# A constant row for the Gram matrix: spread over partitions by a DRAM transfer instead of by matmuls

## The chip, the cores and the metric

The kernel runs on one NeuronCore of a Trainium2 chip. The metric is device time in microseconds (us) of one execution. Names of the engines: PE is TensorE (PEld its weight loads), DVE is VectorE, ACT is ScalarE, POOL is GpSimd, SP is SyncE, which here only issues DMAs. "SPq" in a row of the profile is SyncE's queue issuing one.

## What is computed

The reference is two residual bottleneck blocks, one after the other, on 64 images of 1024 channels and 14 x 14 pixels, in float32:

```
out = relu(bn(conv1x1(x,   w1) + b1, g1, be1))      # 1024 -> 256 channels
out = relu(bn(conv3x3(out, w2) + b2, g2, be2))      # 256 -> 256
out = bn(conv1x1(out, w3) + b3, g3, be3)            # 256 -> 1024
x   = relu(x + softplus(residual_scale) * out)
```

`bn` takes mean and variance of a channel over all images and pixels (12544 values), then scales and shifts.

## The kernel before

`y_all` holds the 256 middle channels of all 12544 pixels in SBUF, as two slots of 128 channels (128 partitions). A block goes through these stages: the first 1x1 convolution and its statistics, the 3x3 convolution (`conv2`, by a Winograd scheme) with its statistics, the Gram stage, and the last 1x1 convolution with the residual, which in the first block is interleaved with the first convolution of the second block. The loop `for b in range(2)` (L1638) runs the last three stages of each block.

**The Gram stage** serves the statistics of the last convolution: mean and variance of its 1024 output channels follow from the 256 x 256 matrix of products of the middle channels, summed over pixels, and from their sums. `gram` (L1119) forms it on TensorE. A matmul sums over partitions, so pixels must stand on partitions; `y` is transposed, 256 pixels at a time, into tiles `zt` (six buffers), and each `zt` takes part in 16 matmuls (the rows cp<-zt and ap<-zt). There are 49 `zt` in a Gram. A constant per channel, `minus_c` (L1641, minus the positive part of the parameter `be2`), is added to `y` first.

- `by_tensor` (L1203): eight of the 49 `zt` come from TensorE: four transposes against `ident` into PSUM (L1208), then one VectorE addition that takes the result out of PSUM and adds the constant (L1215). After the transpose channels lie along the free dimension, so the constant is needed as a row of 256 values, the same in all 128 partitions: `c_row`.
- `by_vector` (L1221): the other 41 are transposed by VectorE in 32 x 32 blocks (L1224). For that the pixels are first moved between groups of 32 partitions: `less` subtracts the constant in place (L1166), then `move` issues DMAs of 80 or 96 KB from SyncE and GpSimd (L1187) and `stay` copies the parts that keep their partitions on ScalarE. The moves go to three buffers `homes` in turn.

**How `c_row` is made before.** `center_row` (L1194) multiplies `minus_c`, broadcast along the free dimension, by the identity, one matmul per slot, which gives the row in all partitions of a PSUM tile of the tag "ax"; ScalarE copies it to SBUF. After the first `by_tensor`, `busy(psum, "ax", 1)` issues one filler matmul of 448 columns.

**The order.** Within an engine the order of the work around this place is the program's: a call of `tc.keep_in_program_order` pins an instruction behind the one traced before it on its engine. Instructions that aren't pinned are placed by the framework's scheduler as soon as it takes them for ready. `pairs` (L1231) sets the order of the Gram: it normalises the first pixels, makes the row, and then, between one `by_tensor` and the next, normalises, subtracts and moves the rest by a list written out by hand. Its first steps on VectorE are: normalise two slices of 256 pixels, `zt` 0, normalise 512 pixels, `zt` 1, subtract from the first moved piece (the moves follow), `zt` 2.

On SyncE, ahead of the Gram, stand the loads of weights: `load_w3` (L170, 1 MB) in both blocks, and `load_w1` (L144, 1 MB in four pieces) in the first block only, for the second block's first convolution.

**Memory.** Tiles come from pools. A pool whose memory another pool held before waits, by default, for all that used the earlier pool; with `reuse_waits="tile"` each tile waits only for what lay at its own place. `homes` are tiles of the pools that later hold `x`; the third one, `homes[2]`, comes from the pool `last_x_{b}`.

Of the kernel before, what the change touches and what calls it, by code (L numbers as in the profile page):

```python
# [38 lines left out]
FP = mybir.dt.float32  # L39
AF = mybir.ActivationFunctionType  # L40
ALU = mybir.AluOpType

P = 128
N, C, H, W = 64, 1024, 14, 14
HW = H * W
M = 256
CS = C // P
MS = M // P
# [42 lines left out]
def bottlenecks(ctx: ExitStack, tc: tile.TileContext, x, w1s, w2s, w3s, pars, out):  # L91
    nc = tc.nc
# [3 lines left out]
    dram = ctx.enter_context(tc.tile_pool(name="dram", bufs=1, space=bass.MemoryType.DRAM))  # L96
# [76 lines left out]
    def matmul(*args, **kw):  # L173

        tc.keep_in_program_order(nc.tensor.matmul(*args, **kw))  # L175

    def busy(psum, tag, n, with_=None):

        v = ident if with_ is None else with_
        for i in range(n):  # L180
            matmul(psum.tile(448, tag), v, v[:, :1].to_broadcast([P, 448]), start=True, stop=True)
# [154 lines left out]
    def act(*args, **kw):  # L336

        tc.keep_in_program_order(nc.scalar.activation(*args, **kw))  # L338
# [247 lines left out]
    def norm_vector(s, y, aff):  # L586

        scale, shift = aff
        tc.keep_in_program_order(
            nc.vector.tensor_scalar(y, y, scale[:, s : s + 1], shift[:, s : s + 1], ALU.mult, ALU.add)  # L590
        )
        tc.keep_in_program_order(nc.vector.tensor_scalar(y, y, 0.0, None, ALU.max))
# [523 lines left out]
            )  # L1116
        return ps

    def gram(psum, pool, homes, aff, minus_c, beside):  # L1119

# [66 lines left out]
                )  # L1189
                tc.keep_in_program_order(ins)  # L1190

        c_row = pool.tile([P, M], FP, tag="c_row", name="c_row")

        def center_row():  # L1194

            ps = psum.tile(M, "ax")
            for s in range(MS):
                matmul(
                    ps[:, s * P : (s + 1) * P], minus_c[:, s : s + 1].to_broadcast([P, P]), ident, start=True, stop=True
                )  # L1200
            act(c_row, ps, AF.Copy)

        def by_tensor(a):  # L1203
            tp = psum.tile(CH * M)
# [26 lines left out]
        def pairs():  # L1231

            for a in 0, px:
                norm_vector(1, y_all[:, 1, a : a + px], aff)
                normed(a, a + px, (0,))
            normed(2 * px, 4 * px, (0,))
            center_row()
            rest = [(piece, s) for piece in still for s in range(MS)]
            (second, end), half = still[1], sum(still[1]) // 2
            for n, a in enumerate(a for piece in still for a in range(*piece, px)):  # L1240
                yield by_tensor(a)
                if n == 0:
                    busy(psum, "ax", 1)
                    norm_vector(1, y_all[:, 1, 2 * px : 4 * px], aff)
                    normed(*moved[0])
                elif n == 1:
                    less(*moved[0])
                    move(0)
                    normed(second, end, (0,))
                    normed(second, half, (1,))  # L1250
                elif n == 3:
                    norm_vector(1, y_all[:, 1, half:end], aff)
                    normed(*moved[1])
                elif n == 4:
                    less(*moved[1])
                    move(1)
                    normed(*moved[2])
                elif n == 5:
                    less(*moved[2], both[:1])
                    stay(1)  # L1260
                elif n == 6:
                    less(*moved[2], both[1:])
                    normed(*moved[3])
                elif n == 7:
                    move(2)
                    stay(2)
            for k, (a, e) in enumerate(moved):
                for i in range((e - a) // px):
                    yield by_vector(k, i)
                    if i in (1, 3) and k and k + 2 < len(moved):  # L1270
                        less(*moved[k + 2], both[i // 2 : i // 2 + 1])
                        if i == 3:
                            move(k + 2)
                            if k + 3 < len(moved):
                                normed(*moved[k + 3])
                            stay(k + 2)
                    elif i in (0, 5) and k > 1 and rest:
                        piece, s = rest.pop(0)
                        less(*piece, (s,))
            assert not rest  # L1280
# [302 lines left out]
    ident = keep.tile([P, P], FP, tag="ident", name="ident")  # L1583
# [12 lines left out]
    with tc.tile_pool(name="first", bufs=1) as one, tc.tile_pool(  # L1596
        name="first_x", bufs=2
    ) as x_left, ExitStack() as scope:
        xpools = x_right, x_left
        psum = Psum(scope, ["ps"], ps=4, ay=2)  # L1600
# [4 lines left out]
        for b in range(2):  # L1605
            p = keep.tile([P, NPAR], FP, tag=f"par{b}", name=f"par{b}")
# [31 lines left out]
    for b in range(2):  # L1638
        pb = par[b]
        minus_c = keep.tile([P, MS], FP, tag="minus_c", name="minus_c")  # L1640
        nc.vector.tensor_scalar(minus_c, pb[:, BE2 : BE2 + MS], 0.0, -1.0, ALU.max, ALU.mult)  # L1641
        stats2 = keep.tile([P, MS, 1 + PARTS, nc.vector.BN_STATS_DIM], FP, tag="stats2", name=f"stats2_{b}")
        with tc.tile_pool(name=f"conv2_{b}", bufs=1, reuse_waits="tile") as pool, ExitStack() as scope:
            border.go_on(Psum(scope, ["l"], l=2, m=2), pool, stats2)

        if b == 0:
            x_right, x_scope = right_pool("last_x_right")
        with tc.tile_pool(name=f"last_{b}", bufs=1) as one, tc.tile_pool(
            name=f"last_x_{b}", bufs=2 if b == 0 else 5
        ) as x_left:  # L1650
            xpools = (x_right, x_left) if b == 0 else (x_left, x_left)
            w3 = load_w3(one, b)
            if b == 0:
                w1 = load_w1(one, b + 1, nc.sync)
            aff = affine(aggregate(stats2, 0), pb, G2, BE2)
            with ExitStack() as scope:
                if b == 0:
                    psum = Psum(scope, ["cy", "ay", "cx", "cy", "ay"], cy=2, ay=2)
                else:
                    psum = Psum(scope, ["cy", "cx"], cy=2, cx=2, cp=2)  # L1660
                with tc.tile_pool(name=f"gram_{b}", bufs=1) as pool:
                    def x_tile(name, t=0):
                        return xpools[t].tile([P, CS * PX], FP, tag="x", name=name)


                    ws = sums_tile(one, 2 - b)
                    homes = [x_tile("home"), x_tile("home") if b else ws.rearrange("p i n -> p (i n)"), x_tile("home", 1)]

                    made_c, made_a = [], []
                    beside = {NPX // (CH * P) - 10: lambda: made_c.append(combine_w3(w3, ws[:, 0]))}  # L1670
                    if b == 0:
                        beside[NPX // (CH * P) - 4] = lambda: made_a.append(combine_w1(w1, ws[:, 1]))
                    grams = gram(psum, pool, homes, aff, minus_c, beside)

                    made = [conv3(psum, 0, 0, w3, "cx" if b else "ay")]
                    mv3 = small.tile([P, CS, nc.vector.BN_AGGR_DIM], FP, tag="mv3", name="mv3")
                    conv3_stats(psum, pool, grams, w3, mv3, ("cy", "cp", "cy", "cp" if b else "cx"), homes[2])
                made.append(conv3(psum, 0, 1, w3, "cx" if b else "ay"))
                tags = ("cy", "cp") * 2 if b else ("cy", "cx", "cy")
                made += [conv3(psum, 0, 2 + i, w3, tag) for i, tag in enumerate(tags)]  # L1680
                if b == 0:
                    psum.cycle = itertools.cycle(["ay", "ay", "cy"])
                aff = affine(mv3, pb, G3, BE3, conv_bias=B3)
                for a in aff:
                    nc.vector.tensor_scalar(a, a, sps[b], None, ALU.mult)
                xs = [load_x(xpools[t % 2], b, t, run=tc.keep_in_program_order) for t in range(2 if b == 0 else 5)]
                later = None if b else []
                residual(psum, xs[0], b, 0, w3, aff, made, later)
                weights = made_a + made_c
                with tc.tile_pool(name=f"rest_{b}", bufs=1) as pool:  # L1690
                    if b == 1:
                        final(psum, pool, x_left, xs, w3, *weights, aff)
                        return
                    stats1 = stats_tile(MS, f"stats1_{b + 1}")
                    border = Border(b + 1, stats1, x_scope)
                    fused(psum, pool, xpools, xs, *weights, aff, par[b + 1], stats1, border, later)
# [40 lines left out]
```

## Time and profile before

| | us |
|---|---|
| three runs | 1922.47, 1921.18, 1922.40 |
| median | 1922.40 |
| profiled execution, its time | 1922.36 |
| its span, from the first to the last instruction | 1920.6 |
| TensorE busy in the span | 1903.6 |
| the first Gram's first `zt` (L1215) starts at | 587.66 |
| the second Gram's first `zt` starts at | 1541.86 |

A row of the timeline has the start and the length in us, engine, line, operation, the tile written and the tiles read, the shape, and how often it is repeated in the row; in square brackets stand the idle time ahead of it and what ended that. A row of waits has who waited for whom, the total in us, how often, and the longest. Fp32 matmuls appear as two passes each. A row of DMA issues has the tile written and read, the queue, the count, the size of one and the median time from issue to landing in us. A row of windows has the window, its length, the busy time of PE, PEld, DVE, ACT and POOL (with instruction counts), the granted TensorE clock as a share, the busy share of the 16 DMA engines, and GB/s.

### The profile page before, as it was taken

The numbers are of one execution on the slowest core, as the hardware profiler recorded it, in microseconds if no ns is written. First come the engines' busy times: TensorE is split into PE (matmuls) and PEld (weight loads), VectorE is DVE, ScalarE is ACT, GpSimd is POOL, SyncE is SP. The second block draws the span as 40 slices with busy tenths as digits, with TensorE's granted clock in tenths as the row PEclk, the third lists the DMA queues.
The fourth block names the chain that finished last, engine by engine and source line by source line (L and its number), as shares of the span: only waits on it lengthen the run. The fifth ranks groups of instructions, "written<-read, shape, count | busy, mean of one in ns | idle before, by whom it ended". The sixth has DMA issues, their size and how long they took to land.

```text
span 1920.6 us, 28737 instructions
## 1 busy us (share of the span) xinstructions
PE 1903.6 (99%) x10236; PEld 1598.3 (83%) x10236; DVE 1547.1 (81%) x2509; ACT 1085.6 (57%) x2152; POOL 565.5 (29%) x678
## 2 busy tenths in 40 slices
PE   9999999999999999999999999999999999999999
PEld 5555557999998799999999999989999987555555
DVE  5787767999998866676776767789999986888886
ACT  2222214677778255555555555556777682666665
POOL 0111100211204133433433333302121041666664
PEclk9999999999999999999999999999999999999999
DMA  7767644787856544444444444358778466889998
GB/s 290 274 241 279 218 154 155 195 223 212 216 168 172 192 159 169 169 168 181 178 179 168 168 169 178 124 179 204 216 209 221 141 171 240 292 325 337 337 341 300
DMA packets 198527, 408.77 MB, mean 213 GB/s; under 512 B 37104, under 2 KB 175024, under 8 KB 181872
## 3 DMA queue, kind: packets, MB, share of 16 engines
q1 hardware_dynamic: 159712, 321.85, 48.9%
q0 software_dynamic: 33056, 34.03, 8.6%
q10 hardware_dynamic: 5616, 51.06, 6.4%
q8 instruction: 81, 1.33, 0.3%
q14 instruction: 62, 0.51, 0.1%
HBM read 263.75 MB, written 115.34 MB: 197 GB/s over the span
## 4 chain that ended last, share of the span: by engine, by line
PE 90%; DVE 5%; DMA 2%; issue 1%; SPq 1%; POOL 1%; ACT 1%; DVEq 0%; ACTq 0%; POOLq 0%
PE cy L175 17%; PE ay L175 17%; PE columns L175 13%; PE cp L175 10%; PE ap L175 9%; PE m L175 7%; PE l L175 6%; PE cx L175 5%; PE ax L175 4%; PE ps L175 1%; DMA home<-y 1%; SPq L1187 1%; DVE zt L1224 1%; DVE y L1166 1%; DMA x<-in_x 1%
## 5 line engine op out<-in xcount | busy, mean ns | idle before, releaser
L338 ACT ACTIVATE cu<-cy,scale 128x196 f32<-128x196 f32 (+1 forms) x552 | 256.7, 474 | 278.0 <-PE cy L175 272.8
L175 PE MATMUL columns<-v,ub 128*128 128x224 f32 (+1 forms) x1536 | 302.4, 338 | 0.8 <-ACT columns L338 0.8
L338 ACT ACTIVATE x<-x,shift 128x392 f32<-128x392 f32 x452 | 255.0, 613 | 72.7 <-POOL x L530 53.6
L175 PEld LDWEIGHTS columns<-v,ub 128*128 128x128 f32 x1536 | 269.2, 188 | 5.7 <-ACT columns L338 1.5
L504 DVE SCALAR_TENSOR_TENSOR x<-cp,scale,x 128x196 f32<-128x196 f32 (+1 forms) x368 | 178.1, 484 | 96.6 <-PE cp L175 95.2
L175 PE MATMUL cy<-ct,ws 128*128 128x196 f32 (+1 forms) x736 | 221.8, 383 | 1.2 <-ACT cu L338 1.2
L175 PE MATMUL ay<-at,ws 128*128 128x196 f32 (+1 forms) x768 | 212.8, 382 | 0.2 <-ACT au L338 0.2
L525 POOL TENSOR_TENSOR x<-x,cu 128x196 f32<-128x196 f32 (+1 forms) x184 | 160.0, 870 | 171.7 <-ACT cu L338 163.9
L530 POOL TENSOR_TENSOR x<-x,cu 128x392 f32<-128x392 f32 x124 | 125.9, 1015 | 191.3 <-DVE x L504 191.3
L175 PEld LDWEIGHTS ay<-at,ws 128*128 128x128 f32 x768 | 139.2, 190 | 35.0 <-ACT au L338 0.8
L175 PEld LDWEIGHTS cy<-ct,ws 128*128 128x128 f32 x736 | 133.4, 190 | 36.4 <-ACT cu L338 4.2
L175 PE MATMUL l<-diffs,ub 128*128 128x224 f32 (+1 forms) x768 | 149.8, 337 | 3.7 <-issue 2.6
L551 POOL TENSOR_TENSOR x<-x,cu 128x392 f32<-128x392 f32 x120 | 122.0, 1017 | 86.2 <-DVE x L504 66.1
L175 PE MATMUL m<-sums,ua 128*128 128x224 f32 (+1 forms) x752 | 146.2, 337 | 0.5 <-DVE sums L667 0.4
L175 PEld LDWEIGHTS l<-diffs,ub 128*128 128x128 f32 x768 | 134.2, 189 | 6.0 <-issue 3.3
L338 ACT ACTIVATE au<-ay 128x196 f32<-128x196 f32 (+1 forms) x140 | 53.4, 382 | 146.4 <-PE ay L175 146.0
L504 DVE SCALAR_TENSOR_TENSOR x<-cx,scale,x 128x196 f32<-128x196 f32 (+1 forms) x184 | 89.1, 484 | 56.7 <-PE cx L175 56.7
L175 PEld LDWEIGHTS m<-sums,ua 128*128 128x128 f32 x752 | 131.3, 189 | 2.3 <-DVE sums L667 1.7
L175 PE MATMUL cy<-y,w 128*128 128x196 f32 (+1 forms) x408 | 125.3, 393 | 0.0
L175 PE MATMUL cx<-y,w 128*128 128x196 f32 (+1 forms) x400 | 122.6, 391 | 0.0
L175 PE MATMUL cp<-y,ws 128*128 128x196 f32 (+1 forms) x368 | 113.6, 390 | 0.2 <-DVE x L504 0.2
L965 POOL DMA_DIRECT2D y<-f x24 | 30.8, 1490 | 274.4 <-DVE f L889 272.5
(239 smaller groups left out, 3996.9 us busy)
## 6 DMA issues: line engine op xcount, KB each, us to landing
x<-in_x SPq DMA_DIRECT2D x62, 1568.0 KB, 6.8
ub<-u SPq DMA_DIRECT2D x92, 768.0 KB, 5.4
x<-mid SPq DMA_DIRECT2D x32, 1568.0 KB, 8.4
mid<-x ACTq DMA_DIRECT2D x31, 1568.0 KB, 5.1
out<-x SPq DMA_DIRECT2D x123, 392.0 KB, 5.9
ua<-u SPq DMA_DIRECT2D x92, 256.0 KB, 3.1
u<-y POOLq DMA_DIRECT2D x48, 256.0 KB, 6.8
home<-y SPq DMA_DIRECT2D x70, 96.0 KB, 3.7
```

What stands on the lines that cost most here:

```text
L175: tc.keep_in_program_order(nc.tensor.matmul(*args, **kw))
L338: tc.keep_in_program_order(nc.scalar.activation(*args, **kw))
L504: nc.vector.scalar_tensor_tensor(v, bank, self.scale[:, o : o + 1], v, ALU.mult, ALU.add)
L525: nc.gpsimd.tensor_add(self.part(1, 1), self.part(1, 1), u3)
L530: nc.gpsimd.tensor_add(v, v, self.u12)
L551: nc.gpsimd.tensor_add(v, v, self.u12[:, i * self.n : (i + 1) * self.n])
L965: nc.gpsimd.dma_start(out=out_rows[3][:, o], in_=fa[:, o, :full], accum_op=ALU.add)
L1166: tc.keep_in_program_order(nc.vector.tensor_scalar(y, y, minus_c[:, s : s + 1], None, ALU.add))
L1187: ins = queue.dma_start(out=x[32 * i : 32 * i + 32, :, j], in_=y_all[32 * j : 32 * j + 32, :, a + i * run : a + i * run + run])
L1224: nc.vector.transpose(zt[:, :, 1 : M + 1].rearrange("p b (n c) -> p b n c", c=32), x[:, :, i * CH * 32 : (i + 1) * CH * 32].rearrange("p n ...
```

## The change

The row is no longer made by TensorE and ScalarE. At the head of each block, right after `minus_c`, GpSimd issues a DMA that writes the 256 values to DRAM in channel order. In `gram`, SyncE issues a DMA that reads these 1 KB once for each of the 128 partitions; it is pinned to the program's order. The row goes to the first 256 columns of `homes[2]`, not to a tile of its own. The filler matmul after the first `by_tensor` goes too. The pool `last_x_{b}`, from which `homes[2]` comes, gets `reuse_waits="tile"`.

```diff
-    def gram(psum, pool, homes, aff, minus_c, beside):
+    def gram(psum, pool, homes, aff, minus_c, c_dram, beside):
...
-        c_row = pool.tile([P, M], FP, tag="c_row", name="c_row")
-
-        def center_row():
-
-            ps = psum.tile(M, "ax")
-            for s in range(MS):
-                matmul(
-                    ps[:, s * P : (s + 1) * P], minus_c[:, s : s + 1].to_broadcast([P, P]), ident, start=True, stop=True
-                )
-            act(c_row, ps, AF.Copy)
+        c_row = homes[2][:, :M]
+        tc.keep_in_program_order(
+            nc.sync.dma_start(out=c_row, in_=bass.AP(c_dram.tensor, c_dram.offset, [[0, P], [1, M]]))
+        )
...
             normed(2 * px, 4 * px, (0,))
-            center_row()
...
                 if n == 0:
-                    busy(psum, "ax", 1)
                     norm_vector(1, y_all[:, 1, 2 * px : 4 * px], aff)
...
         nc.vector.tensor_scalar(minus_c, pb[:, BE2 : BE2 + MS], 0.0, -1.0, ALU.max, ALU.mult)
+        c_dram = dram.tile([M], FP, tag=f"c{b}", name=f"c{b}")
+        nc.gpsimd.dma_start(out=c_dram.rearrange("(s p) -> p s", p=P), in_=minus_c)
...
-            name=f"last_x_{b}", bufs=2 if b == 0 else 5
+            name=f"last_x_{b}", bufs=2 if b == 0 else 5, reuse_waits="tile"
         ) as x_left:
...
-                    grams = gram(psum, pool, homes, aff, minus_c, beside)
+                    grams = gram(psum, pool, homes, aff, minus_c, c_dram, beside)
```

## The prediction

> **What bounds the kernel now.** I read the busy times first, then TensorE's waits, then the timeline of each engine around the two places where the row is made (the first Gram at 586 us, the second at 1540 us), then SyncE's queue and the DMA windows there.
>
> ```profile
> PE 1903.6 (99%) x10236; PEld 1598.3 (83%) x10236; DVE 1547.1 (81%) x2509; ACT 1085.6 (57%) x2152; POOL 565.5 (29%) x678
> ...
> PE ax L175 <- ACT c_row L338: 1.0, 2, 0.5
> ...
> PE cp L175 <- DVE zt L1224: 0.7, 3, 0.3
> ```
>
> TensorE has work for 1903.6 of 1920.6 us, so a change counts only by how it moves TensorE. Its whole wait for the row is 1.0 us in two waits: what the change can win there is of that order. But the row also holds up VectorE, which starts the moves of `y` for the rest of the Gram. The first Gram, TensorE and then VectorE:
>
> ```profile
> 586.11 0.61 PE L175 MATMUL ax<-ident,minus_c 128*128 128x128 f32 x4
> 586.55 0.60 PE L1208 MATMUL cy<-ident,y 128*128 128x128 f32 x4
> 587.63 1.02 PE L175 MATMUL ax<-ident 128*128 128x448 f32 x2 [0.48 <-ACT c_row L338]
> 588.49 0.60 PE L1208 MATMUL ay<-ident,y 128*128 128x128 f32 x4
> 589.02 0.55 PE L175 MATMUL cp<-zt 128*64 128x193 f32 x4
> ...
> 586.74 0.29 DVE L592 TENSOR_SCALAR y<-y 128x256 f32<-128x256 f32 x1
> 587.66 0.69 DVE L1215 TENSOR_TENSOR zt<-cy,c_row 128x512 f32<-128x512 f32 x1 [0.63 <-ACT c_row L338]
> ```
>
> The reader should see that VectorE is free at 587.03 and the transposes end at 587.15, but the first `zt` starts only at 587.66, when ScalarE has copied the row. The second Gram is the same picture 954.2 us later (`zt` at 1541.86). What the new transfer meets, first SyncE's queue, then the landing times of the 1024 KB and the last two 256 KB weight loads of the first Gram and of the one load of the second, then DMA windows (last two columns: DMA share, GB/s):
>
> ```profile
> 581.02 0.36 SPq L170 DMA_DIRECT2D w<-in_w  x1
> 581.42 2.09 SPq L144 DMA_DIRECT2D w<-in_w  x4
> ...
> w<-in_w SPq DMA_DIRECT2D x1, 1024.0 KB, 4.8
> ...
> w<-in_w SPq DMA_DIRECT2D x2, 256.0 KB, 5.9
> ...
> w<-in_w SPq DMA_DIRECT2D x1, 1024.0 KB, 5.0
> ...
> 587.00:588.00 1.00, 0.52 (x3) 0.30 (x2) 0.37 (x2) 1.00 (x3) 0.00 (x0) 1.00 0.95 367
> 588.00:589.00 1.00, 1.00 (x6) 0.50 (x4) 0.97 (x3) 1.00 (x2) 0.00 (x0) 1.00 0.17 66
> ...
> 1539.00:1540.00 1.00, 1.00 (x4) 0.45 (x3) 0.89 (x7) 0.30 (x1) 0.53 (x6) 1.00 0.41 172
> ```
>
> At the first Gram 2 MB of weights (`w3`, and `w1` in four pieces) keep the DMA engines full until 588.2; at the second only `w3` is loaded, and they are idle from 1539.4. And what stands later in each Gram:
>
> ```profile
> 601.95 3.08 DVE L1224 STREAM_TRANSPOSE zt<-home 128x512 f32<-128x512 f32 x5 [1.05 <-DMA ws<-y]
> ...
> 602.72 0.55 PE L175 MATMUL cp<-zt 128*64 128x193 f32 x4 [0.28 <-DVE zt L1224]
> ...
> 1561.47 1.30 DVE L1224 STREAM_TRANSPOSE zt<-home 128x512 f32<-128x512 f32 x2 [2.95 <-DMA home<-y]
> ...
> 1562.24 0.55 PE L175 MATMUL cp<-zt 128*64 128x193 f32 x4
> ```
>
> The `zt` made from moved pixels wait for DMAs, and TensorE catches up with them: at 602.72 by 0.28 us, at 1562.24 by 0.29 us (the matmuls of before start at 1561.73 and would go on at 1561.95). So each Gram moves by what the moves move by.
>
> **What the Trainium skill says.** "DMA: Bandwidth & Descriptors", section "Queues, rings and completion order": SyncE owns one ring on each DMA engine, and on each engine descriptors are consumed in ring order. The trace agrees: the last 256 KB piece lands 5.9 us after its issue, longer than the 1 MB load issued first on an idle ring (4.8). The same page, "Rules for kernel authors": a strided last dimension takes one descriptor per element; that is the new write of 256 floats. No such transfer is in this trace. "TensorE: Matmul & The Clock Gate", Part 1: after an idle window of about 3.4 us the clock halves until a busy window has passed. Here gaps of up to 1.6 us (the wait list's longest) left the granted clock at 1.00; a longer gap isn't shown.
>
> **The change part by part.**
>
> *Removed.* Per Gram: two fp32 matmuls in four passes (586.11 to 586.55), the ScalarE copy (363 ns), the 448-column filler in two passes (587.63 to 588.49). With the row at hand the second Gram would run so: transposes wait for VectorE's first `y` (ends 1540.57) instead of the matmuls, so 1540.6 to 1541.2; VectorE is free at 1541.23 (0.94 + 0.29); first `zt` at about 1541.27 against 1541.86, a gain of 0.59. Everything behind it on VectorE up to the subtraction (L1166) that releases the moves is back to back, so the moves start 0.59 earlier. TensorE itself gains more: second transposes 1541.3 to 1541.9, Gram at 1542.0 against 1543.21, 1.2 us. But that surplus ends in the DMA wait at 1561.47, where the DMA share has been 0.9 to 1.07 since the moves began: there only the 0.6 of the moves is left.
>
> *Added, the DRAM write.* On GpSimd's queue, 256 elements of 4 bytes. GpSimd's issues here take 0.54 (L1187) to 1.49 us (L965); I take 1.5. `minus_c` is ready at 10.1 us, where GpSimd is idle from 1.3 to 51.7, and for the second block at 631.8, where at most the last moves (the last issued at 632.88) stand behind it and then nothing until 670.28. Those moves may slip by 1.5 us; SyncE's last ones, issued at 633.70 to 635.5, land after them anyway. Cost 0; if that cover were gone, 1.5 us on one Gram.
>
> *Added, the row transfer.* 128 rows of 1 KB. It is pinned on SyncE behind what was traced there before it, and that is `w3`, and in the first block all four pieces of `w1`. Its own wait for the write is long over. `reuse_waits="tile"` lets it wait only for what lay at its place; the last conv2 reads are over at 583, so it costs and gains nothing beyond SyncE's order.
>
> First Gram: issue at 583.5 (581.42 + 2.09), ring busy until 588.2; 128 KB at 350 GB/s is 0.37 us; the last weight piece landed at 583.1 + 5.9 = 589.0, some 0.8 after its data, so the row lands at 588.2 + 0.37 + 0.8 = 589.4. First `zt` at 589.4 against 587.66: **1.75 us later**. Bounds: 588.9 if it lands with the weights (+1.3), 590.4 if 1 KB rows go at a third of the rate (+2.8). Behind the waiting `zt` on VectorE stand the norm of the next slice and the subtraction before the moves, so all moves start 1.75 later. TensorE, waiting for `zt`, starts Gram at 590.15 against 589.02, 1.1 later, but meets the DMA wait again: the moved `zt` comes at 601.95 + 1.75, its matmul at 602.72 + 1.73 = 604.45. From there TensorE is without a wait but for 0.17 us, so 1.73 stays.
>
> Second Gram: issue at 1535.65, ring busy until 1539.4, landing 1539.4 + 0.37 + 0.8 = 1540.6. Wanted at 1541.27: 0.67 to spare, so the whole 0.6 is won. Bounds: -0.6 to +0.5 (the row at 1541.6 to 1542.4).
>
> *Moved.* `c_row` in `homes[2]` is overwritten by the third move and by ScalarE's copies, which follow the last `zt` that reads it (600.22 to 600.9; the move from 601.47): 0. ScalarE runs 0.3 us ahead, behind which nothing waits.
>
> **Sum.** The profiled execution took 1922.36 us, 1.76 more than its span and 0.04 under the median of the three runs, 1922.4. 1922.36 + 1.73 - 0.6 = **1923.5**. The gain of one Gram is outweighed by the lateness in the other; next late is the move chain, as now.
>
> **Rivals.**
> - *The row is in time in both Grams* (the transfer slips past the weights, or weights drain sooner). Then both gain 0.6: 1922.36 - 1.2 = 1921.2. For it: the row was made to come early. Against it: the DMA share of 0.95 to 0.99 until 588 and the ring order. 13%.
> - *The late row lets TensorE's clock fall* in the first Gram. TensorE would idle from 587.7 to 590.15, 2.4 us. It decides at 3.4 us (the page's window), that is, a row that lands at 590.4 or later, or at a lower limit than the page's. Then VectorE is 2.8 late and TensorE 2.2; at half clock for one to two windows (3.4 to 6.8 us) it loses another 1.7 to 3.4, say 2.55, which gives 4.75 on TensorE, less the 0.28 it waits at 602.72: 4.45. The second Gram's gain is then 0.1, as its row is 1 us later too. 1922.36 + 4.35 = 1926.7. For it: all 128 rows read the same 1 KB of DRAM, which no row of this trace does. Against it: the 1.6 us gaps. 12%.
> - *Nothing visible*: the row comes with the weights' end in the first Gram (+1.3) and part of it is regained in slack that I don't see: about 1922.5. 10%.
>
> **How the numbers follow.** The forecast's case has 65%, its own range 1922.4 to 1924.7. No change means within 0.2% (3.8 us), which is about what a measurement of this kernel can tell: 1918.6 to 1926.2. The clock case lies mostly above it, 0.11 with some mishap in the order of other instructions; nothing reaches below it but that, 0.02; the rest is 0.87. The range runs from the in-time case, 1921.2, to just short of the clock case, 1926.2. It leaves out the clock case's 11%, the 2%, and the lower half of the in-time case, 6%.
>
> **What would show it.** In the profile after: the row's issue at about 583.5 and 1535.6, its landing about 589.4 and 1540.6 (the second pair 1.73 later, as all of it is); first `zt` at 589.4, waiting for a DMA, in the first Gram, and in the second at 1543.0 (1541.27 + 1.73), waiting for none; the moves 1.75 later in the first and 0.6 earlier (after that shift) in the second; a TensorE gap of 2.4 us with the clock at 1.00. It is wrong if the row is issued ahead of the weights, if a PE clock under 1.00 stands after the gap, or if either Gram's first move shifts by something other than its first `zt` does.

## The result, and the profile after

| | before | after |
|---|---|---|
| median of six runs each | 1922.42 us (1921.18 to 1923.04) | 1930.3 us (1927.8 to 1932.13) |
| profiled execution | 1922.36 | 1931.22 |
| its span | 1920.6 | 1929.4 |

The ratio of after to before is 1.004, with a 95% interval of 1.003 to 1.0051: slower by 7.9 us, outside the range of the prediction. The loss isn't where the prediction worked. The page's busy times and the longest waits of TensorE say so at once (who waited for whom, total in us, how often, the longest):

```profile
PE 1905.9 (99%) x10224; PEld 1598.1 (83%) x10224; DVE 1547.7 (80%) x2509; ACT 1084.6 (56%) x2150; POOL 564.6 (29%) x680
...
PE ay L175 <- DVE at L438: 3.4, 1, 3.4
PE cp L175 <- DVE zt L1209: 2.8, 2, 2.7
PE cp L175 <- DVE zt L1218: 2.7, 2, 2.4
```

TensorE has fewer matmul passes than before (10224 against 10236) and is busy 2.3 us longer: some run at a lower granted clock, as the windows further down show. Its three new waits of over 2 us stand in three places. Only the second, on the `zt` of the late row (L1209), was forecast; the first is at the start of the kernel, 550 us ahead of the row.

**Where the time goes.** Marks in the two timelines, each the start of a named instruction:

| mark | before | after | shift |
|---|---|---|---|
| conv2 of block 1 begins (first ls<-l) | 316.30 | 320.94 | +4.64 |
| `w3` issued ahead of the first Gram | 581.02 | 585.65 | +4.63 |
| first `zt` of the first Gram | 587.66 | 594.18 | +6.52 |
| first `zt` made from moved pixels | 601.95 | 608.38 | +6.43 |
| the first Gram's result is read (g<-cp) | 648.19 | 659.06 | +10.87 |
| `w3` issued ahead of the second Gram | 1535.27 | 1546.12 | +10.85 |
| first `zt` of the second Gram | 1541.86 | 1552.13 | +10.27 |
| the second Gram's result is read | 1602.33 | 1611.73 | +9.40 |
| span | 1920.6 | 1929.4 | +8.8 |

So: +4.63 before any Gram, +1.8 to +1.9 at the head of the first Gram, +4.4 in the rest of it, -1.5 in the second (-0.6 of it at its head), and -0.6 after it (sum +8.8). The terms at the two heads are close to those of the sum on record (+1.73, -0.6). The two large ones stand beside the two DRAM writes.

**The start of the kernel.** The issues of the first 40 us, the loads of `x` before and then after, and the write; then windows, first of before and then of after (last three columns: granted TensorE clock, DMA share, GB/s):

```profile
x<-in_x SPq DMA_DIRECT2D x5, 1568.0 KB, 10.0
...
x<-in_x SPq DMA_DIRECT2D x5, 1568.0 KB, 16.5
...
c<-minus_c POOLq DMA_DIRECT2D x1, 1.0 KB, 12.6
```

```profile
16.00:18.00 2.00, 2.00 (x8) 1.17 (x7) 1.03 (x2) 0.59 (x1) 0.00 (x0) 1.00 0.97 414
18.00:20.00 2.00, 2.00 (x8) 1.17 (x7) 0.00 (x0) 0.00 (x0) 0.00 (x0) 1.00 1.02 433
20.00:22.00 2.00, 2.00 (x8) 1.17 (x7) 0.00 (x0) 0.00 (x0) 0.00 (x0) 1.00 0.95 406
22.00:24.00 2.00, 2.00 (x8) 1.17 (x7) 0.60 (x1) 0.00 (x0) 0.00 (x0) 1.00 0.99 409
...
14.00:16.00 2.00, 2.00 (x8) 1.17 (x7) 2.00 (x4) 0.44 (x1) 0.00 (x0) 1.00 1.77 408
16.00:18.00 2.00, 2.00 (x8) 1.17 (x7) 0.65 (x2) 0.59 (x1) 0.00 (x0) 1.00 1.03 100
18.00:20.00 2.00, 2.00 (x8) 1.17 (x7) 0.00 (x0) 0.00 (x0) 0.00 (x0) 1.00 1.00 138
20.00:22.00 2.00, 2.00 (x8) 1.17 (x7) 0.00 (x0) 0.00 (x0) 0.00 (x0) 1.00 0.69 75
22.00:24.00 2.00, 2.00 (x8) 1.17 (x7) 0.00 (x0) 0.00 (x0) 0.00 (x0) 1.00 0.40 88
```

GpSimd issues the write at 10.02 in 0.87 us, but its 1 KB lands 12.6 us later, and while it is under way all DMA engines of the core together move 75 to 138 GB/s, where before they move 406 to 433 in the same windows. The loads of `x`, which are issued on another queue and share no data with the write, take 16.5 us to land instead of 10.0. Who waits for them: VectorE before, then VectorE and TensorE after:

```profile
23.40 1.79 DVE L437 TENSOR_TENSOR at<-x 128x1568 f32<-128x1568 f32 x1 [5.44 <-DMA x<-in_x]
...
29.88 1.79 DVE L437 TENSOR_TENSOR at<-x 128x1568 f32<-128x1568 f32 x1 [12.21 <-DMA x<-in_x]
...
35.69 4.57 PE L175 MATMUL ay<-at,ws 128*128 128x392 f32 x8 [3.44 <-DVE at L438]
```

VectorE's first `at` comes 6.48 us later. TensorE has work queued for some microseconds, then stands for 3.44.

The trace's records of single packets say what the DMA engines do meanwhile. (A window counts a packet whole where it starts, so a share over 1, as in 14 to 16, means packets that last beyond the window.) The write goes out as 16 packets of 64 bytes, which start between 14.25 and 15.82 and take 0.025 us each. After that it is the packets of the loads of `x`, 12544 bytes each, that last long: of those that start between 14 and 26 us none takes over 0.49 us before, and 33 take over 1 us after, the longest 6.33.

**The end of the first Gram.** The second write is issued at 640.18, when the last moves of `y` are under way. Windows of after, then VectorE and TensorE, which make the Gram's last `zt` from these moves and multiply them:

```profile
644.00:646.00 2.00, 2.00 (x34) 1.82 (x32) 0.67 (x2) 0.00 (x0) 0.00 (x0) 1.00 1.73 55
646.00:648.00 2.00, 2.00 (x34) 1.79 (x30) 0.00 (x0) 0.00 (x0) 0.00 (x0) 1.00 0.94 50
648.00:650.00 2.00, 0.32 (x6) 0.07 (x2) 0.04 (x1) 0.00 (x0) 0.00 (x0) 1.00 0.10 13
650.00:651.00 1.00, 0.28 (x2) 0.28 (x4) 1.00 (x2) 0.00 (x0) 0.00 (x0) 0.85 0.28 50
651.00:652.00 1.00, 1.00 (x10) 0.82 (x10) 1.00 (x3) 0.00 (x0) 0.00 (x0) 0.50 0.80 301
```

```profile
649.96 1.90 DVE L1218 STREAM_TRANSPOSE zt<-home 128x512 f32<-128x512 f32 x3 [5.29 <-DMA home<-y]
...
650.73 0.92 PE L175 MATMUL cp<-zt 128*64 128x193 f32 x4 [2.41 <-DVE zt L1218]
```

The write lands after 8.9 us, at 649.12; the rate is 13 to 55 GB/s for six of them, where before, from 638 to 644, it was 347 to 427. The two moves that SyncE issues behind the write, at 640.46 and 642.04, land at 649.29 and 649.45, just after the write, though the records of the moves' packets end at 644.43; the moves issued ahead of it have landed by 644.55. VectorE waits 5.29 us for the last moved pixels and TensorE 2.41; the clock column then shows half speed.

**The head of the first Gram.** SyncE's issues, then VectorE and TensorE, then windows:

```profile
585.65 0.36 SPq L170 DMA_DIRECT2D w<-in_w  x1
586.06 2.16 SPq L144 DMA_DIRECT2D w<-in_w  x4
588.26 0.43 SPq L1194 DMA_DIRECT2D home<-c  x1
```

```profile
594.18 0.69 DVE L1209 TENSOR_TENSOR zt<-cy,home 128x512 f32<-128x512 f32 x1 [2.51 <-DMA home<-c]
...
594.93 0.55 PE L175 MATMUL cp<-zt 128*64 128x193 f32 x4 [2.65 <-DVE zt L1209]
...
596.20 1.12 PE L1202 MATMUL cx<-ident,y 128*128 128x128 f32 x4
597.25 0.91 PE L175 MATMUL cp<-zt 128*64 128x193 f32 x4
```

```profile
595.00:596.00 1.00, 1.00 (x16) 0.92 (x16) 0.97 (x3) 1.00 (x2) 0.00 (x0) 1.00 0.00 0
596.00:597.00 1.00, 1.00 (x10) 0.72 (x4) 1.00 (x2) 1.00 (x2) 0.00 (x0) 0.54 0.00 0
597.00:598.00 1.00, 1.00 (x8) 0.59 (x8) 1.00 (x3) 1.00 (x2) 0.00 (x0) 0.50 0.00 0
598.00:599.00 1.00, 1.00 (x10) 0.86 (x8) 0.58 (x1) 1.00 (x2) 0.71 (x2) 0.50 0.00 0
599.00:600.00 1.00, 1.00 (x10) 0.66 (x6) 0.00 (x0) 1.00 (x2) 1.00 (x3) 0.75 0.73 164
```

The row is issued behind the weights and lands 5.8 us later; the first `zt` waits for it. That is the picture on record, but for the clock: after a gap of 2.65 us it falls to half, 1.2 us after work resumes, and four `cp` passes take 0.91 us instead of 0.55.

### The profile page after: what moved, and what is told of

It is laid out like the page before. It is cut to its first block, busy times and chain, and to the rows that moved or that the text cites. A ratio compares the mean times of both kernels' runs of the same rounds, so it can differ in the third digit from the quotient of the medians.

```text
span 1929.4 us, 28727 instructions
## 1 busy us (share of the span) xinstructions
PE 1905.9 (99%) x10224; PEld 1598.1 (83%) x10224; DVE 1547.7 (80%) x2509; ACT 1084.6 (56%) x2150; POOL 564.6 (29%) x680
## 4 chain that ended last, share of the span: by engine, by line
PE 90%; DVE 4%; DMA 3%; issue 1%; POOL 1%; SPq 0%; ACT 0%; DVEq 0%; POOLq 0%; ACTq 0%
PE cy L175 17%; PE ay L175 17%; PE columns L175 13%; PE cp L175 11%; PE ap L175 9%; PE m L175 6%; PE l L175 6%; PE cx L175 5%; PE ax L175 4%; DMA x<-in_x 1%; DMA home<-y 1%; POOL home L1187 0%; DVE y L1166 0%; SPq L1187 0%; DMA home<-c 0%
## 5 line engine op out<-in xcount | busy, mean ns | idle before, releaser
L175 PE MATMUL cy<-ct,w 128*128 128x196 f32 (+1 forms) x368 | 111.0, 383 | 0.5 <-ACT cu L338 0.5
```

## The experiments

My theory after seeing the two traces: the write of 256 single floats holds up all DMA traffic while it is under way, and both large terms are its doing. The rivals: the late row is what costs, by the clock that falls behind it; or, as the prediction had it, the write costs only its issue on GpSimd, and something else in the change moved the loads. The first four kernels tell these apart. Where later expectations use letters, L is the theory that small runs which share a stretch of DRAM are taken one after the other, C that the fall of TensorE's clock makes the late row dear, D that the moves of `y` set the pace there and the clock matters little.

**The write alone.** The kernel before, rows by matmul as before, with the two writes added; nothing reads what they write.

```diff
         nc.vector.tensor_scalar(minus_c, pb[:, BE2 : BE2 + MS], 0.0, -1.0, ALU.max, ALU.mult)
+        c_dram = dram.tile([M], FP, tag=f"c{b}", name=f"c{b}")
+        nc.gpsimd.dma_start(out=c_dram.rearrange("(s p) -> p s", p=P), in_=minus_c)
```

> The kernel before with the DRAM writes of the constant added and never read; the row is still made by matmuls. Theory W (the write of 256 single floats jams the DMA engines while x and the moves need them): about +4.6 us by the first Gram and about +4.1 us between the last subtraction of the first Gram and its end, some 1931 us in all; the write lands 9 to 13 us after its issue and the DMA rate falls to some 100 GB/s meanwhile. Theory R (the late row and its TensorE gap are the cost): 1922.4. Theory O (the other order of instructions and waits that came with the new pool mode is the cost): 1922.4.

Measured: 1927.26 us (1926.21 to 1932.44), ratio 1.0033 (1.0021 to 1.0046); some 1931 had been expected. Its two long waits of TensorE:

```profile
PE ay L175 <- DVE at L438: 3.9, 1, 3.9
PE cp L175 <- DVE zt L1224: 2.9, 1, 2.9
```

In its profile (span 1930.7) the shift is +6.59 us when `w3` is issued ahead of the first Gram and +10.78 when that Gram's result is read, without any row to wait for; the writes land 11.9 and 9.0 us after their issue; TensorE waits 3.9 us at the start and 2.9 us at the end of the Gram. So the write alone makes both large terms, and by the medians 5.1 of the 7.9 us; with six runs each, which scatter by 4 to 6 us, the share isn't known more closely.

**The change with the writes later.** Everything as after, but GpSimd issues each write behind the work that was traced before it.

```diff
-        nc.gpsimd.dma_start(out=c_dram.rearrange("(s p) -> p s", p=P), in_=minus_c)
+        tc.keep_in_program_order(
+            nc.gpsimd.dma_start(out=c_dram.rearrange("(s p) -> p s", p=P), in_=minus_c)
+        )
```

> The changed kernel with the two writes pinned behind GpSimd's earlier work, so that they are issued in quieter stages (about 290 us and 1280 us). Theory W: the two stalls of 4.6 and 4.1 us go; what stays is the late row of the first Gram (+1.8 to +2.2) and the gain of the second (-0.6 to -1.4): 1922.5 to 1924. Theories R and O: no change from 1930.

Measured: 1923.36 us (1921.5 to 1923.97), ratio 1.0004 (0.9995 to 1.0013). The writes are now issued at 238.39 and 1244.12, earlier than the 290 and 1280 expected. They are no quicker, they land 13.0 and 11.2 us after that, but TensorE loses nothing there. Windows at the second one:

```profile
1248.00:1250.00 2.00, 1.78 (x11) 1.81 (x12) 1.61 (x4) 0.39 (x1) 0.00 (x0) 1.00 2.07 293
1250.00:1252.00 2.00, 2.00 (x14) 2.00 (x13) 0.81 (x2) 0.34 (x1) 0.00 (x0) 1.00 0.60 70
1252.00:1254.00 2.00, 2.00 (x14) 2.00 (x13) 0.00 (x0) 0.20 (x1) 0.00 (x0) 1.00 0.72 134
```

The rate falls as at the earlier place, and TensorE works through it: it is busy for 15.72 of the 16 us from 1242 to 1258, and for 15.71 of 16 in the same stretch before (1240 to 1256). The late row and the new pool mode are still in this kernel, so neither of them makes the two large terms. What is left is the row's part: at the first Gram

```profile
589.17 0.69 DVE L1209 TENSOR_TENSOR zt<-cy,home 128x512 f32<-128x512 f32 x1 [2.49 <-DMA home<-c]
...
589.91 0.65 PE L175 MATMUL cp<-zt 128*64 128x193 f32 x4 [2.63 <-DVE zt L1209]
```

that is +1.87 us for the first `zt` (it starts 1.51 us later, in a profile that was 0.36 us ahead when `w3` was issued), and at the second Gram the first `zt` is 0.58 us earlier relative to `w3`'s issue. The span is 1.2 us longer than before; the sum on record for these parts is 1.13.

**The same bytes in two runs.** The kernel before with one unread write of 1 KB at the same place in time, from two partitions, each 512 bytes side by side in DRAM.

```diff
+        row = y_all[:MS, 1, NPX // 2 : NPX // 2 + P]
+        nc.vector.tensor_scalar(row, par[0][:MS, BE2 : BE2 + 1].to_broadcast([MS, P]), 0.0, -1.0, ALU.max, ALU.mult)
+        c_dram = dram.tile([M], FP, tag="c0", name="c0")
+        nc.gpsimd.dma_start(out=c_dram.rearrange("(s p) -> s p", p=P), in_=row)
```

> The kernel before with one DMA of the same 1 KB at the same moment (10 us) as the first of the writes, but from two partitions as two runs of 512 B instead of 256 runs of 4 B; it is never read. Theory W (the number of tiny runs is what jams): 1922.4, landing after 3 to 5 us, no stall. Rival W2 (any GpSimd DMA that early, beside the full loads, jams): +4.6, 1927.

Measured: 1923.24 us (1922.22 to 1924.64), ratio 1.0004 (0.9995 to 1.0012). It lands 6.0 us after its issue (3 to 5 were expected) and the rate stays at 414 to 433 GB/s from 16 to 24 us.

```profile
c<-y POOLq DMA_DIRECT2D x1, 1.0 KB, 6.0
```

Neither a write to DRAM at this place nor GpSimd's queue is the cost; the form of the write is.

**The writes later and the row first.** As the kernel with the later writes, and SyncE issues the row ahead of `w3` and `w1`. For that the `homes` tiles are taken from their pools there, and the row's transfer in `gram` goes.

```diff
             xpools = (x_right, x_left) if b == 0 else (x_left, x_left)
+            at = [xpools[t].tile([P, CS * PX], FP, tag="x", name="home") for t in ((0, 1) if b == 0 else (0, 0, 1))]
+            tc.keep_in_program_order(
+                nc.sync.dma_start(
+                    out=at[-1][:, :M], in_=bass.AP(c_dram.tensor, c_dram.offset, [[0, P], [1, M]])
+                )
+            )
             w3 = load_w3(one, b)
...
-        nc.sync.dma_start(out=w, in_=w3s[b])
+        tc.keep_in_program_order(nc.sync.dma_start(out=w, in_=w3s[b]))
```

> The changed kernel with the writes pinned as in the other run and the row's transfer issued ahead of the weight loads on SyncE. Theory W with the row theory of the prediction: both Grams gain 0.6 to 1.4 us, 1920 to 1921.2. If the row's lateness is not what holds the first Gram: no difference from the run with the writes pinned alone.

Measured: 1920.92 us (1919.13 to 1921.68), ratio 0.999 (0.9982 to 0.9999). SyncE's issues at the first Gram:

```profile
581.58 0.35 SPq L1647 DMA_DIRECT2D home<-c  x1
582.41 0.35 SPq L170 DMA_DIRECT2D w<-in_w  x1
582.81 2.36 SPq L144 DMA_DIRECT2D w<-in_w  x4
```

and VectorE's first `zt`, with no wait ahead of it:

```profile
587.69 0.69 DVE L1206 TENSOR_TENSOR zt<-cy,home 128x512 f32<-128x512 f32 x1
```

The row lands 3.0 us after its issue (3.4 in the second Gram). The first `zt` gains 0.59 us in the first Gram (+0.62 where conv2 begins, +0.03 at `zt`) and 0.59 in the second (-0.46 where the first Gram's result is read, -1.05 at `zt`). The clock stays at 1.00, and the span is 2.1 us shorter.

The next runs ask what in the form of the write costs, and what the clock's fall costs.

**Half as many runs.** As the write alone, but in the order `"(p s) -> p s"`, in which each partition's two floats lie side by side: 128 runs of 8 bytes.

> The kernel before with the unread write added, but in the order that leaves the two floats of a partition side by side in DRAM: 128 runs of 8 B instead of 256 of 4 B. Theory N (each run to DRAM costs the engine a fixed time, whatever lies next to it): half the jam, landing after some 6 to 8 us, x late by 3 us instead of 6.5 to 7.6, which the slack of TensorE hides: 1922 to 1924. Theory L (partial writes that share a line of DRAM wait for each other): nothing is eased, since the same lines are written: 1927 or more.

Measured: 1922.63 us (1921.73 to 1923.43), ratio 1.0001 (0.9993 to 1.001). About half the disturbance (the table below has it), and TensorE doesn't stand for it: the first `at` is 2.65 us late, within what TensorE has queued. Theory N foresaw this, theory L did not.

**As many runs, far apart.** 256 floats, each 512 bytes from the next.

```diff
+        c_dram = dram.tile([M * P], FP, tag=f"c{b}", name=f"c{b}")
+        nc.gpsimd.dma_start(out=c_dram.rearrange("(s p k) -> p s k", p=P, k=P)[:, :, 0], in_=minus_c)
```

> The kernel before with the unread write added, each of the 256 floats 512 B from the next in DRAM. Theory L (partial writes that share a line wait for each other): no jam, landing after 3 to 5 us, 1922.4. Theory N (fixed time per run): the same as the unread dense write, 1927 to 1932, landing 9 to 13 us.

Measured: 1923.17 us (1921.95 to 1923.96), ratio 1.0006 (0.9997 to 1.0014). The windows at the start, with 256 floats under way:

```profile
16.00:18.00 2.00, 2.00 (x8) 1.17 (x7) 0.59 (x2) 0.59 (x1) 0.00 (x0) 1.00 0.99 420
18.00:20.00 2.00, 2.00 (x8) 1.17 (x7) 0.00 (x0) 0.00 (x0) 0.00 (x0) 1.00 1.06 452
20.00:22.00 2.00, 2.00 (x8) 1.16 (x7) 0.00 (x0) 0.00 (x0) 0.00 (x0) 1.00 0.92 389
```

No disturbance: this is as theory L has it and against theory N, so neither holds as it was put. It isn't the number of small runs: it is that they lie close together in DRAM.

**How close?** As the last one, with `k` of 4, 16 and 2 in place of 128: floats 16, 64 and 8 bytes apart.

> The kernel before with the two writes of 256 floats that nobody reads, each float 16 bytes from the next in DRAM. Theory L (runs that share a stretch of DRAM are taken one after the other, some 30 ns each): a stretch of 64 bytes or more still holds four or more floats, so the transfer jams as when the floats lie side by side: it lands 9 to 13 us after its issue, the DMA rate falls under 180 GB/s between 16 and 24 us, and the time is 1926 to 1929. If only floats side by side within 16 bytes disturb one another, or the total span of DRAM decides: lands in 5 to 7 us, no fall of the rate, 1922 to 1923.

> The same with each float 64 bytes from the next. Theory L with a shared stretch of 64 bytes or less: no jam, lands 5 to 6 us after its issue, the rate stays over 350 GB/s, 1922 to 1923. With a stretch of up to 512 bytes (eight floats in each): a jam as with the floats side by side, 1925 to 1929.

> The kernel before with the two writes of 256 floats that nobody reads, each float 8 bytes from the next in DRAM. If runs disturb one another only where they share 16 bytes (two runs in each here, as with the 128 runs of 8 bytes, and some 30 ns for every run), 256 runs jam as long as the floats side by side: landing 9 to 13 us after the issue, the DMA rate low for 7 to 8 us, 1926 to 1929. If the jam grows with the runs in a longer stretch of DRAM (64 bytes hold 16 of the floats side by side, 8 of the 8-byte runs, 4 of the floats 16 bytes apart), it is about half as long: landing 6 to 8 us after the issue, rate low for 3 to 4 us, 1922.3 to 1924. If only runs that touch disturb one another: lands in 4 to 6 us, no fall, 1922 to 1923.

Measured, with all forms of the write together. "Lost" is worked out: the GB/s of the five windows of 2 us from 16 to 26, summed, taken from the same sum before (2133), times 2 us, over the mean before (426.6). "Long packets" counts the packets of the loads of `x` that start between 14 and 26 us and take over 1 us (none before). Both are from one profile of each kernel.

| the write of 1 KB | runs in 64 bytes of DRAM | lands after, first and second write | lost, us of transfer | long packets | ratio to before (95%) |
|---|---|---|---|---|---|
| 256 floats side by side | 16 | 11.9, 9.0 us | 5.5 | 37 | 1.0033 (1.0021 to 1.0046) |
| 128 x 8 bytes side by side | 8 | 7.5, 5.6 | 2.4 | 19 | 1.0001 (0.9993 to 1.001) |
| 256 floats, 8 bytes apart | 8 | 7.4, 5.6 | 2.2 | 25 | 1.0008 (0.9999 to 1.0017) |
| 256 floats, 16 bytes apart | 4 | 6.1, 4.1 | 0.5 | 6 | 1.0 (0.9992 to 1.0009) |
| 256 floats, 64 bytes apart | 1 | 6.1, 4.7 | 0.0 | 0 | 0.9998 (0.999 to 1.0007) |
| 256 floats, 512 bytes apart | under 1 | 5.9, 4.7 | 0.1 | 0 | 1.0006 (0.9997 to 1.0014) |
| 2 x 512 bytes (one write) | - | 6.0 | 0.0 | 0 | 1.0004 (0.9995 to 1.0012) |

My idea of some 30 ns for each run that shares a stretch fails: floats 16 bytes apart should have lost as much as floats side by side if the stretch is 64 bytes, and floats 8 bytes apart twice as much as 128 runs of 8 bytes if it is 16. What fits these seven forms is the density: 256 runs 8 bytes apart and 128 runs of 8 bytes side by side have the same number of runs in a stretch of DRAM and lose the same, though one has twice the runs and twice the span. With the density halved, the loss more than halves (5.5, 2.3, 0.5). The write's own 16 packets don't tell the forms apart: they take 0.025 us each with the floats side by side and with the floats 512 bytes apart. The medians of the kernels with the smaller losses lie within 1.7 us of before; for the two that lose 2.2 and 2.4, conv2 of block 1 begins no later than before (-0.09 and -0.84 us), so TensorE's queued work covers the loss at the start.

**Work in the gap.** As the kernel with the later writes, with three filler matmuls behind the first transposes, so that TensorE doesn't idle for the late row.

```diff
                 if n == 0:
+                    busy(psum, "ax", 3)
                     norm_vector(1, y_all[:, 1, 2 * px : 4 * px], aff)
```

> The run with the writes pinned, plus three filler matmuls behind the first transposes, some 2.3 us of TensorE work in the place of the 2.6 us for which it waits for the row. The row stays late. Theory D (the moves, started late behind the late row, hold the first Gram, and the fall of the clock costs nothing): the clock stays at 1.00 and the time stays, 1923.4 within 0.5. Theory C (the fallen clock costs as the prediction's rival had it): 1 to 2 us less than the run with the writes pinned.

Measured: 1925.23 us (1923.72 to 1927.25), ratio 1.0015 (1.0009 to 1.0022). The clock stays at 1.00 in the first Gram. But the fillers also run in the second Gram, where the row is in time: there they put the second transposes off, and the first `zt` from moved pixels comes 1.25 us later than before, counted from the issue of `w3`, where without the fillers it comes 0.26 us earlier. So its total says nothing on the clock. Once more, with the fillers under `if first_gram:`, passed as `b == 0`:

> The pinned writes with the three filler matmuls in the first Gram alone, where the row comes late; the second Gram is as in pinned_write. Both theories expect TensorE's granted clock at 1.00 after the late row. Theory D (the moves set the pace there, so the fall of the clock costs little): 1922.8 to 1923.5, within 0.6 of pinned_write. Theory C (the fall of the clock after the gap is what makes the late row dear): 1 to 2 us less than pinned_write, 1921.4 to 1922.4.

Measured: 1922.66 us (1921.54 to 1924.33), ratio 0.9998 (0.999 to 1.0006). The clock is 1.00 throughout. The first `zt` from moved pixels is as late as without fillers (+1.77 and +1.78 against where `w3` is issued), and the first Gram's result 1.37 late instead of 1.95. So the moves carry the lateness, with or without the fall of the clock, as theory D has it. What the fall itself costs isn't settled: 0.6 us by these two profiles, but two profiles of one kernel, the one with the row first, differ by 0.9 at that mark; 1.3 us by the medians, each against its own runs of before (+1.2 and -0.1), with intervals that overlap. The median, 1922.66, lies between the ranges of the two theories.

**The best version again.**

> The same kernel as the run with the pinned writes and the row ahead of the weights, timed again for a closer interval: 1920.9, a ratio of 0.9993 to the kernel before, if the first timing (0.999) holds.

Measured: 1920.49 us (1919.61 to 1921.93), ratio 0.9991 (0.9983 to 0.9999), on another chip than the first time. With the first run (0.999), it is faster than before by 0.1%, less than the 0.2% that was taken as the bound of what can be told; two intervals that both end below 1 make it likely all the same.

## Why the prediction was wrong

**The step that failed** is "Added, the DRAM write", priced at "Cost 0; if that cover were gone, 1.5 us on one Gram". It priced the issue on GpSimd's queue and asked who stands behind it on that queue. The issue took 0.87 and 0.73 us and nothing stands behind it on that queue. What it left out is the transfer's own time on the DMA engines and what else is under way there: at 10 us the loads of `x` that the first convolution starts on, at 640 us the last moves of the Gram. For those it said that SyncE's moves "land after them anyway", which looked at the order of issue; the two moves that SyncE issued behind the write landed 8.8 and 7.4 us after their issue, where before they took 5.0 and 3.6. In the profiled execution of after the two writes cost 4.6 and about 4.4 us. By the medians both together cost 1927.26 - 1922.16 = 5.1 us when added alone, and about 7.9 - 1.2 = 6.7 in the change, whose other part costs 1.2. The executions differ: the profiled one of the write alone is the longest of its six (1932.44 of 1926.21 to 1932.44), so its shifts are the upper end of what the write costs alone.

The number of elements was in the text, with the Trainium skill, page "DMA: Bandwidth & Descriptors", section "Rules for kernel authors": a strided last dimension takes one descriptor per element. The sentence after it said that no such transfer is in the trace. The row's transfer was given bounds on both sides; the write, just as new to the trace, was given none beyond its issue. A warning, though no price, stands on the same page: its "Specifications" say that below 512 bytes a transfer is made as read-modify-write; such a write may then be more work than its bytes. The runs agree only in part: 4 bytes at a time do no harm where the floats lie 64 or 512 bytes apart; closeness is needed as well. That the cause is a read-modify-write isn't shown.

**Right: the late row of the first Gram.** Issue 2.61 us after that of `w3` (2.5 on record), landing 5.8 us later (5.9), first `zt` 1.89 us late by its own (1.75), the first `zt` from moved pixels 1.80 (1.75). The kernel with the later writes shows the same by itself: 1.87 and 1.78.

**Right: the second Gram.** First `zt` 0.58 us earlier (0.59). (Of the bounds given there, a row at 1541.6 would leave a gain of 0.3, not 0.6.) By the end of the Gram the gain is between 0.1 and 1.5 us in the profiles of the five kernels that have the row in time there and no fillers; 0.6 was on record. The write alone, which changes nothing there, shows 0.7 too, and the write with floats 8 bytes apart 1.5 the other way, so what is left at the end of the Gram isn't shown by single profiles.

**Right in the sum without the write:** 1922.36 + 1.73 - 0.6 = 1923.5 on record, 1923.36 measured with the writes where nobody waits. That close a hit is partly luck: the interval of this run is -1.0 to +2.5 us against before, and what it confirms best is the shift of each first `zt`. And the rival "the row is in time in both Grams", 1921.2, is what the row-first kernels gave, 1920.9 and 1920.5, with 0.59 us won in each Gram.

**Wrong, and small as far as it shows: the clock.** The forecast "TensorE gap of 2.4 us with the clock at 1.00" didn't hold. The Trainium skill's page "TensorE: Matmul & The Clock Gate", Part 1, has the clock halve after an idle window of about 3.4 us; here it fell after gaps of 2.41, 2.63, 2.65, 2.91, 3.44 and 3.89 us (gaps of up to 1.6 us left it at 1.00, and none lay between), so gaps shorter than the page's figure do it, and the bound taken from it was too high. The length of the slow stretch does agree with the page's window: in the windows of 1 us behind the gap of 2.65, the clock's missing shares are 0.46, 0.50, 0.50 and 0.25, in sum 1.71 us of full speed, or 3.4 us at half. The rival priced it at 2.55 us on TensorE and nearly all of it on the path (its 4.45 should read 4.47, which changes nothing). It measures 1.7 on TensorE; how much of that stays isn't settled, 0.6 to 1.3 us by the two measures above, since TensorE then catches up with the moves, which are as late without the fall.

Still open: why runs close together in DRAM hold up the other transfers. The records of packets place the time: the engines are occupied not by the write's own packets, which are over in 0.025 us each, but by packets of other transfers that stand open behind them, up to 6.33 us at the first place. What these wait for, no record shows. Whether the stretch that matters is 32 or 64 bytes isn't told apart either, nor whether neighbours in one packet or in different packets disturb one another.

## What to carry to other kernels

A small write to DRAM is priced by its runs and by where they lie as well, not by its bytes or its issue alone: ask whether its destination is one element per run and the runs are neighbours, and if so, which transfers are on the path during the 10 us after its issue. Where such a write can't be avoided, it can be put where no one waits for a DMA. Floats laid out 16 bytes or more apart, or 512 bytes side by side from each of two partitions, cost the kernel nothing measurable as writes; a row read back from such floats, or the cost of bringing the values together first, wasn't measured. And the transfer that is needed first goes into the queue ahead of the bulk loads: the same row landed in 3.0 to 3.4 us there and in 5.8 behind 2 MB of weights.

## What the runs showed of the hardware that was not expected

- A write of 1 KB as 256 neighbouring floats took 9.0 to 15.5 us to land in these runs and cost the core some 5.5 to 6.3 us of its whole DMA rate at the first place; floats 16 bytes apart cost 0.5, 64 bytes apart nothing.
- The disturbance begins with the write's first packets, some 4 us after its issue (issued at 10.02, packets from 14.25 on, 408 GB/s from 14 to 16, then 100), and it hits transfers of another queue: the loads of `x` and the last moves are SyncE's, the write is GpSimd's.
- TensorE's clock fell to half after each of the six gaps of 2.4 us and more in these profiles, up to 1.2 us after work had resumed, and stayed there for 3.41 us each time.
